# A two-layer graph attention and mixture-of-experts kernel: layer 1's sum over two experts issued in two halves, the planning and padding of the last slots issued in four pieces, and layer 1's two-expert slots moved forward among the last

## The chip, the cores and the metric

The kernel runs on one core of a Trainium2 chip. The metric is the time of one execution on the device in microseconds (us), and the time before is the median of three runs. A profile, taken by the hardware profiler in one further execution, gives the start and length of each instruction, what ended each wait, and the clock that TensorE was granted. The engines are PE (TensorE, matrix products), DVE (VectorE), ACT (ScalarE), POOL (GpSimd) and SP (SyncE, which here does nothing but start transfers).

## The reference, cut to what matters

The input is x, 128 graphs of 64 nodes with 256 features (8192 tokens), and an adjacency matrix of 64 x 64 for each graph. Two layers follow each other, and each has two halves:

```
x = x + elu(attention(layernorm(x), adj))    # inside each graph of 64 nodes
t = layernorm(x)
p = top-2 of the router's 8 scores of t, weights normalised over the two
x = x + (t, in layer 0 alone) + sum over the two experts e of p[e] * ffn_e(t)
```

The experts' hidden width is 256 with gelu in layer 0 and 512 with relu in layer 1. All is float32. Each token goes through only two of eight experts, and which two is known only when the router has run. So the kernel sorts tokens into one list per expert in DRAM as it goes.

## The kernel before

**Blocks.** Tokens are handled in blocks of 512, 16 in a layer, 32 in all. A block runs through `attend` (attention) and then `route` (router and scatter of its rows into the experts' lists). Both are Python generators: every `yield` marks a point at which the program's main loop may turn to something else. `a(i, n)` takes n steps of block i's `attend`, `r(i, n)` n steps of its `route`.

**Slots.** The experts' work goes in slots of 256 rows of one list. A slot has three steps: `x()` turns its rows round on PE (px, L764) and copies them (xT, DVE L768); `h()` is the first layer (ph, PE L846, then ACT L855); `y()` the second (py, PE L877, then DVE L884 adds the bias into ys). py has a single buffer, so the next `y()` on PE waits for DVE's L884 of the slot before. In layer 0 POOL then scatters ys to DRAM (L893). In layer 1 `weighted()` lets ACT scale it (L919) and POOL adds it onto the output rows in DRAM (L922); two adds that could meet on one row must not overlap, so each slot's adds wait until those of the slot before have landed.

**Plans.** After a block's rows are in the lists, `plan` works out on DVE which experts have 256 rows waiting and hands out four slots. At three points, block 8 and block 15 of layer 0 and block 15 of layer 1, the lists end: `fill_up` appends 256 rows of padding to each of the eight lists (eight SP transfers, L526), and `rests` (L604 to L669, some 35 small DVE instructions) plans the remainder as twelve slots: eight of one expert, and seven lists' ends of 128 rows, taken in twos: three slots of two experts (called pair slots here) and a last one of a single half. A pair slot needs two sets of weights and its two halves are added one after the other. The twelve are taken in the order whole, whole, pair, whole, whole, pair, whole, whole, pair, whole, whole, single.

**Buffers and queues.** Weights of experts (wc) have four buffers, and SP loads them ahead (`ahead`, `weights`). Fetches of a slot's rows (`fetch`) go on SP too. Every engine runs its own instructions in the order in which the program issued them; for SP, PE, DVE and ACT that order is exactly the order of these lines (`manual_schedule`), so the main loop (from L1037 on) decides it. One pass of the loop carries block n = t+1 through attention, block t through routing, block t+2 through the start of attention, and four slots through h, y and x.

**Where the first parts stand.** In layer 1 the first step of `attend` adds the two experts' results of layer 0 to xs, with eight scalar_tensor_tensor instructions (L267, 128 x 256 each). In the loop this step of block t+2 comes as `a(t + 2)` just before a `y()`, and behind that stands `a(n)`, block n's normalisation of the softmax (erc and ee, L334 and L335), whose result PE turns round as pp (L339). From pp come pT_bd (DVE L341, ACT L342) and po (PE L348). In the last step of `route` stand `plan`, `fill_up` and `rests` together.

Of the kernel before, what the change touches and what calls it, by code (L numbers as in the profile page):

```python
# [9 lines left out]
I32 = mybir.dt.int32  # L10
# [6 lines left out]
P = 128  # L17
# [3 lines left out]
E = 8  # L21
TT = 4
# [5 lines left out]
ST = SL // P  # L28
# [7 lines left out]
def adj_ffn_kernel(  # L36
# [34 lines left out]
    nc = tc.nc  # L71
    N = x.shape[0]
    NT = N // P
    NB = N // TB
# [6 lines left out]
    SF = SR + E - 1  # L81
# [44 lines left out]
    for g in range(2):  # L126
        r = slice(g * NG, (g + 1) * NG)
# [132 lines left out]
    def attend(l, b, blk):  # L260

        name = f"g{l}_{b}"
        xs, yb, ai = blk["in"]
        if l > 0:
            for t in range(TT):
                for k in range(2):
                    nc.vector.scalar_tensor_tensor(  # L267
                        xs[:, t, :],
                        yb[:, t, k * D : (k + 1) * D],
                        cs[:, b * TT + t, k : k + 1],  # L270
                        xs[:, t, :],
                        ALU.mult,
                        ALU.add,
                    )
        yield
        stats = ln_stats(xs, name)

        m = work.tile([P, TT, NG], F32, tag="cap", name=f"cap_{name}")
# [123 lines left out]
    def route(l, b, blk):  # L402
# [106 lines left out]
        if b - (CUT if b >= CUT and l == 0 else 0) >= LAG:  # L509
            slots.take(l, b, SB, plan(l, f"p{l}_{b}", SB))  # L510
        if b == NB - 1 or (l == 0 and b == CUT - 1):
            fill_up(l, b)
            slots.take(l, b, SF, rests(l, f"p{l}_{b}r"), True)


    def fill_up(l, b):

        bi = small.tile([P, E], I32, tag="bi", name=f"bi{l}_{b}")
        nc.vector.tensor_copy(bi, base[l])
        wr = []  # L520
        for e in range(E):
            r = nc.values_load(
                bi[0:1, e : e + 1], engines=[SP], min_val=0, max_val=E * CAP - SL,
                skip_runtime_bounds_check_because="a list ends within its room",
            )
            ins = nc.sync.dma_start(  # L526
                out=lists[l][bass.ds(r, SL), :].rearrange("(t p) d -> p t d", p=P),
                in_=pad[:, :, 0 : ROW[l]],
            )
            unordered(f"lists{l}", ins)  # L530
            wr.append(ins)
        written[l].append(wr)
        filled[l].extend(wr)
# [71 lines left out]
    def rests(l, name):  # L605

        lf = small.tile([P, E], F32, tag="lf", name=f"lf_{name}")  # L610
        nc.vector.scalar_tensor_tensor(lf, done[l][:, 0:E], -float(SL), base[l], ALU.mult, ALU.add)
        ns = waiting(lf, name)
        nc.vector.tensor_scalar(lf, lf, float(P), None, ALU.subtract)
        pairs = waiting(lf, f"{name}p")
        cc = small.tile([P, 2 * E], F32, tag="cc", name=f"cc_{name}", bufs=1)
        nc.vector.tensor_scalar(cc[:, 0:E], pairs, 2.0, None, ALU.mult)
        nc.vector.tensor_tensor(cc[:, E : 2 * E], ns, pairs, ALU.subtract)
        cum = small.tile([P, 2 * E], F32, tag="cum2", name=f"cum_{name}", bufs=1)
        summed_up(cum[:, 0:E], cc[:, 0:E], f"{name}p")
        summed_up(cum[:, E : 2 * E], cc[:, E : 2 * E], name)  # L620
        nc.vector.tensor_scalar(
            cum[:, E : 2 * E], cum[:, E : 2 * E], cum[:, E - 1 : E], None, ALU.add
        )
        np_ = small.tile([P, 1], F32, tag="np", name=f"np_{name}", bufs=1)
        nc.vector.tensor_scalar(np_, cum[:, E - 1 : E], 0.5, None, ALU.mult)

        at = small.tile([P, SF], F32, tag="hat", name=f"hat_{name}", bufs=1)
        nc.vector.scalar_tensor_tensor(at, sful, np_, snum, ALU.min, ALU.add)
        ge = work.tile([P, SF, 2 * E + 1], F32, tag="ee", name=f"ge_{name}")
        nc.vector.tensor_tensor(  # L630
            ge[:, :, 0 : 2 * E],
            cum.unsqueeze(1).to_broadcast([P, SF, 2 * E]),
            at.unsqueeze(2).to_broadcast([P, SF, 2 * E]),
            ALU.is_le,
        )
        vs = small.tile([P, SF], F32, tag="vs", name=f"vs_{name}", bufs=1)
        nc.vector.tensor_reduce(vs, ge[:, :, 0 : 2 * E], AX.X, ALU.add)

        w = small.tile([P, 2 * E + 1], F32, tag="w2", name=f"w_{name}", bufs=1)
        nc.vector.tensor_tensor(w[:, 0 : 2 * E], cc, cum, ALU.subtract)  # L640
        for i in range(2):
            wi = w[:, i * E : (i + 1) * E]
            nc.vector.scalar_tensor_tensor(wi, done[l][:, 0:E], 2.0, wi, ALU.mult, ALU.add)
        nc.vector.tensor_tensor(w[:, E : 2 * E], w[:, E : 2 * E], cc[:, 0:E], ALU.add)
        nc.vector.tensor_scalar(
            w[:, 2 * E : 2 * E + 1], done[l][:, E : E + 1], 2.0, -2.0 * SR, ALU.mult, ALU.add
        )
        nc.vector.tensor_tensor(
            ge,
            eidx.unsqueeze(1).to_broadcast([P, SF, 2 * E + 1]),  # L650
            vs.unsqueeze(2).to_broadcast([P, SF, 2 * E + 1]),
            ALU.is_equal,
        )
        nc.vector.tensor_tensor(
            ge, ge, w.unsqueeze(1).to_broadcast([P, SF, 2 * E + 1]), ALU.mult
        )
        us = small.tile([P, SF], F32, tag="us", name=f"us_{name}")
        nc.vector.tensor_reduce(us, ge, AX.X, ALU.add)
        tab = small.tile([P, 2, SF], I32, tag="tab", name=f"tab_{name}", bufs=5)
        nc.vector.tensor_tensor(tab[:, 0, :], us, at, ALU.add)  # L660
        es = small.tile([P, SF], F32, tag="es", name=f"es_{name}", bufs=5)
        nc.vector.tensor_scalar(es, vs, float(E), -float(E), ALU.is_ge, ALU.mult)
        nc.vector.tensor_tensor(es, es, vs, ALU.add)
        nc.vector.tensor_scalar(tab[:, 1, :], es, float(E - 1), None, ALU.min)
        took(l, ns, name)
        bu = small.tile([P, E], F32, tag="bu", name=f"bu_{name}")
        nc.vector.tensor_scalar(bu, done[l][:, 0:E], float(SL), None, ALU.mult)
        base[l] = bu
        return es, tab, sum(written[l], [])  # L669

    def fetch(sl, name):

# [16 lines left out]
    class Slots:  # L689
# [10 lines left out]
        def take(self, l, b, n, plan, rest=False):  # L700
            es, tab, ins = plan

            slots = [[(s, slice(0, ST))] for s in range(SR if rest else n)]
            if rest:
                for i, s in enumerate(range(SR, n, ST)):
                    of = [(s + t, slice(t, t + 1)) for t in range(min(ST, n - s))]
                    slots.insert((ST + 1) * i + ST, of)
            for of in slots:
                self.all.append(
                    {"l": l, "of": of, "es": es, "tab": tab, "filled": ins, "wc": [],  # L710
                     "part": part(b), "sums": list(summed), "rest": rest,
                     "st": of[-1][1].stop}
                )
                self.need.extend((len(self.all) - 1, s) for s, _ in of)
# [260 lines left out]
    def a(i, n=1):  # L975
        if there(i):
            for _ in range(n):
                next(blks[i]["a"], None)

    def r(i, n=1):  # L980
# [12 lines left out]
    load(2)  # L993
    load_router()
    load(FIRST)
    a(0, 2)
    make_gw(0)
    a(0)
    a(1, 2)
    token2 = counted("token2", [P, NT], [[2 * P, NT]], 0, 2)  # L1000
    token = counted("token", [P, NT], [[P, NT]], 0, 1)
    place = counted("place", [P, ST], [[P, ST]], 0, 1)
    att = lambda b: [(a, b)] * 9 + [(a, b, 2), (a, b)]
    chains = [
        (0, att(0)[3:] + [(r, 0)] * 10),
        (1, att(1)[2:] + [(r, 1)] * 10),
        (2, att(2) + [(r, 2)] * 9),
        (8, att(3) + [(r, 3)] * 2),
        (12, [(a, 4)] * 3),
    ]  # L1010
    turn = 0
    while any(c for _, c in chains):
# [20 lines left out]
            for l in range(2):  # L1033
                rest_of_lists(l)
        turn += 1
    r(2)
    slots.fetch()  # L1037
    slots.ahead()
    for t in range(FIRST, len(blks)):
        n = t + 1  # L1040
        more = slots.nf - slots.ny > SB or len(slots.all) - slots.ny > SB
        if t + 3 != NB:
            load(t + 3)
        a(n)
        h()
        x()
        a(n)
        r(t - 1)
        a(n)
        h()  # L1050
        r(t)
        slots.fetch()
        if more:
            x()
        a(n)
        r(t)
        if t + 2 != NB:
            a(t + 2)
        y()
        a(n)  # L1060
        (h if more else x)()
        r(t)
        a(n)
        y()
        a(t + 2, 1 + (t + 2 == NB))
        if more:
            x()
        a(n)
        r(t)
        x()  # L1070
        h()
        a(n)
        if more:
            y()
        x()
        a(n)
        h()
        r(n)
        y()
        a(t + 2)  # L1080
        r(t)
        r(t)
        y()
        slots.fetch()
        x()
        r(n)
        r(t)
        if t + 3 == NB:
            load(t + 3)
# [4 lines left out]
    while slots.ny < len(slots.all):  # L1094
        h()
        x()
        y()
        slots.fetch()
    slots.weighted()

# [46 lines left out]
```

## Time and profile before

| what | value |
|---|---|
| median of 3 runs | 1414.73 us (1414.56 to 1415.14) |
| profiled execution | 1416.24 us |
| its span, first to last instruction | 1414.4 us |
| mean granted clock of PE | 0.941 |
| PE, DVE, ACT, POOL busy | 1215.8, 872.8, 646.5, 742.8 us |
| PE's wait for ee (L335) in front of pp | 38.0 us, 19 times |
| PE's wait for sm (L301) in front of pe | 15.6 us, 4 times |
| PE's longest wait in front of ph (L846) | 7.4 us |
| weights of an expert, 512 KB, issue to landing | 4.9 us |
| DMA traffic | 311.69 MB, 220 GB/s |

A row of the timeline reads: start, length, engine, line, operation, result<-operands, partitions x elements, how many instructions are drawn together, and in brackets how long the engine stood idle before and what ended it. A list of waits has: who waited, for whom, us in all, times, the longest. The row PEclk gives the granted clock in tenths for 40 equal slices of the span.

### The profile page before, as it was taken

How to read it: one execution, taken by the hardware profiler on the slowest of the kernel's cores; microseconds unless marked ns; L12 is line 12 of the kernel's file. 1: busy time of each engine (PE TensorE's matmuls, PEld its weight loads, DVE VectorE, ACT ScalarE, POOL GpSimd, SP SyncE). 2: the span in 40 equal slices, each digit the busy share in tenths (PEclk: the TensorE clock that was granted, in tenths of full speed). 3: DMA queues.
4: the chain of work that ended last, by engine and by line, in shares of the span. 5: the costliest groups of instructions: out<-in, count | busy, mean ns of one | idle time of the engine just before them, and what ended most of it. 6: DMA issues, size and time to landing. Idle time of an engine off the chain costs nothing. (4 is left out here: it accounts for less than half of the span.)

```text
span 1414.4 us, 22289 instructions
## 1 busy us (share of the span) xinstructions
PE 1215.8 (86%) x6240; PEld 1046.3 (74%) x6240; DVE 872.8 (62%) x3390; ACT 646.5 (46%) x1550; POOL 742.8 (53%) x729
## 2 busy tenths in 40 slices
PE   6756799879899887888899999999999999799992
PEld 4645677768787776776788787887878887688882
DVE  3565677877667777767766656766567654523330
ACT  5534556546556544544544454344544444233330
POOL 3153576646666654566545664556645556533323
PEclk9767899989999998999999999999999999999997
DMA  6626567797777978778789887798877777888883
GB/s 198 184 86 191 184 206 235 222 264 235 229 236 222 305 253 249 235 220 273 253 246 265 228 244 202 207 264 228 249 189 216 216 193 205 246 226 227 223 225 34
DMA packets 262829, 311.69 MB, mean 220 GB/s; under 512 B 40615, under 2 KB 219950, under 8 KB 262704
## 3 DMA queue, kind: packets, MB, share of 16 engines
q1 hardware_dynamic: 219552, 225.02, 52.7%
q0 software_dynamic: 43152, 85.24, 22.5%
q8 instruction: 50, 0.82, 0.3%
q14 instruction: 75, 0.61, 0.1%
HBM read 212.25 MB, written 99.75 MB: 221 GB/s over the span
## 5 line engine op out<-in xcount | busy, mean ns | idle before, releaser
L877 PE MATMUL py_s<-wc_s,hT_s 128*128 128x256 f32 x1648 | 402.3, 394 | 31.6 <-issue 22.1
L846 PE MATMUL ph_s<-xT_s,wc_s 128*128 128x256 f32 (+1 forms) x1760 | 384.8, 371 | 19.2 <-DVE xT_s L768 9.1
L877 PEld LDWEIGHTS py_s<-wc_s,hT_s 128*128 128x128 f32 x1648 | 314.4, 197 | 81.6 <-issue 24.8
L922 POOL DMA_INDIRECT out_dram<-ys_s,to_s x135 | 213.2, 1579 | 289.5 <-ACT ys_s L919 150.6
L846 PEld LDWEIGHTS ph_s<-xT_s,wc_s 128*128 128x128 f32 x1760 | 317.6, 192 | 64.1 <-DVE xT_s L768 15.4
L499 POOL DMA_INDIRECT lists<-tn_r,ix_r x256 | 248.8, 972 | 97.0 <-issue 65.8
L855 ACT ACTIVATE hT_s<-ph_s,wc_s 128x256 f32<-128x256 f32 (+1 forms) x440 | 174.5, 456 | 143.5 <-PE ph_s L846 90.6
L884 DVE TENSOR_TENSOR ys_s<-py_s,wc_s 128x512 f32<-128x512 f32 (+1 forms) x149 | 97.3, 653 | 171.2 <-PE py_s L877 170.3
L893 POOL DMA_INDIRECT res<-ys_s,to_s x142 | 144.4, 1017 | 106.7 <-DVE erc_g L334 36.5
L768 DVE COPY xT_s<-px_s 128x512 f32<-128x512 f32 (+1 forms) x140 | 95.3, 681 | 93.4 <-PE px_s L764 93.2
L290 PE MATMUL pw_g<-gw,xt_g 128*128 128x258 f32 x512 | 126.2, 397 | 20.0 <-DVE xt_g L255 13.1
L290 PEld LDWEIGHTS pw_g<-gw,xt_g 128*128 128x128 f32 x512 | 96.6, 197 | 41.3 <-issue 13.0
L919 ACT ACTIVATE ys_s<-ys_s,cf_s 128x256 f32<-128x256 f32 x135 | 61.3, 499 | 104.1 <-DVE ys_s L884 103.9
L240 ACT ACTIVATE tn_r<-xb_g,nb_r,rs_r 128x256 f32<-128x256 f32 x128 | 66.4, 589 | 87.3 <-DVE nb_r L238 87.3
L240 ACT ACTIVATE xn_g<-xs,nb_g,rs_g 128x256 f32<-128x256 f32 x128 | 66.4, 589 | 75.4 <-DVE nb_g L238 75.3
L764 PE MATMUL px_s<-ident,xg_s 128*128 128x128 f32 x554 | 86.9, 281 | 6.4 <-DMA xg_s<-lists 3.7
L764 PEld LDWEIGHTS px_s<-ident,xg_s 128*128 128x128 f32 x554 | 71.3, 147 | 20.2 <-DMA xg_s<-lists 3.8
L279 POOL TENSOR_SCALAR cap_g<-adj 128x256 f32<-128x256 int32 x32 | 35.7, 1116 | 85.8 <-DMA adj<-in_adj_dram 51.7
L348 PE MATMUL po_g<-wh_g,pT_bd 128*128 128x256 f32 x256 | 69.4, 418 | 8.3 <-ACT pT_bd L342 6.8
L297 ACT COPY wh_g<-pw_g 128x258 f32<-128x258 f32 x128 | 47.7, 374 | 58.6 <-PE pw_g L290 57.9
L419 PEld LDWEIGHTS pl_r<-rw,xt_r 128*128 128x128 f32 x512 | 68.8, 209 | 5.3 <-ACT xt_r L257 2.9
L342 ACT COPY pT_bd<-pp_g 64x256 f32<-64x256 f32 x32 | 11.6, 363 | 131.1 <-DVE pT_bd L341 131.0
(503 smaller groups left out, 1612.6 us busy)
## 6 DMA issues: line engine op xcount, KB each, us to landing
wc_s<-in_w_dram SPq DMA_DIRECT2D x142, 512.0 KB, 4.9
wc_s<-in_w_dram SPq DMA_DIRECT2D x156, 256.0 KB, 4.2
xg_s<-lists SPq DMA_DIRECT2D x64, 260.0 KB, 3.2
xg_s<-lists SPq DMA_DIRECT2D x64, 258.0 KB, 4.4
yb<-res SPq DMA_DIRECT2D x16, 1024.0 KB, 12.3
wc_s<-bcat SPq DMA_DIRECT2D x78, 129.0 KB, 4.0
wc_s<-bcat SPq DMA_DIRECT2D x71, 130.0 KB, 5.7
xs<-in_x_dram SPq DMA_DIRECT2D x16, 512.0 KB, 6.2
```

The costliest lines, as they stand in the source:

```text
L240: nc.scalar.activation(outs(t), xb[:, t, :], AF.Identity, bias=nb[:, t : t + 1], scale=rs[:, t : t + 1])
L290: nc.tensor.matmul(pw, lhsT=xt[:, k, t * P : (t + 1) * P], rhs=gw[l][:, k, :], start=(k == 0), stop=(k == KD - 1),)
L348: nc.tensor.matmul(po[h][:, j, :], lhsT=pT[:, 2 * h + j, :], rhs=wh[:, 2 * h + j, 0:D], start=True, stop=True,)
L499: ins = nc.gpsimd.indirect_dma_start(out=lists[l], out_offset=bass.IndirectOffsetOnAxis(ap=ix[:, k, t : t + 1], axis=0), in_=tn[:, t, 0 : ...
L764: nc.tensor.transpose(px[:, c, t * P : (t + 1) * P], xg[:, t, c * P : (c + 1) * P], ident)
L768: nc.vector.tensor_copy(xT[:, :, 0 : st * P], px[:, :, 0 : st * P])
L846: nc.tensor.matmul(ph[:, j, r], lhsT=w[:, o : o + P], rhs=xT[:, c, r], start=(c == 0), stop=(c == KD - 1),)
L855: nc.scalar.activation(hT[:, f + j, r], ph[:, j, r], AF.Gelu if l == 0 else AF.Relu, bias=w[:, OB1[l] + f + j : OB1[l] + f + j + 1],)
L877: nc.tensor.matmul(py[:, t, :], lhsT=hT[:, f, t * P : (t + 1) * P], rhs=w[:, O2[l] + f * D : O2[l] + (f + 1) * D], start=(f == 0), stop=(f ...
L884: nc.vector.tensor_tensor(ys[:, r, :], py[:, r, :], w[:, OB2[l] : OB1[l]].unsqueeze(1).to_broadcast([P, r.stop - r.start, D]), ALU.add,)
L893: ins = nc.gpsimd.indirect_dma_start(out=res[sl["part"]], out_offset=self.row(sl, t), in_=ys[:, t, :], in_offset=None, bounds_check=2 * N - 1,
L922: ins = nc.gpsimd.indirect_dma_start(out=out, out_offset=self.row(sl, t), in_=ys[:, t, :], in_offset=None, compute_op=ALU.add,)
```

## The change

The first step of `attend` is split: the sum's eight instructions come in two groups of four with a `yield` between. Where the next block is one of layer 1, the loop issues block n's erc and ee between the groups, ahead of the `y()` that followed the sum; the second group follows that `y()`.

`fill_up` now takes two experts at a time, and `rests` yields four times, so that planning and padding come in four pieces, each a DVE piece and two fills on SP. The loop takes these pieces with `r(t - 1)` at five more places, spread over the pass that follows the block's routing; the slots are handed out after the fourth. After the last block a `r(len(blks) - 1)` stands behind each `y()`.

In layer 1 the twelve slots are now taken in the order whole, pair, whole, pair, whole, pair, whole, whole, whole, whole, whole, single. In layer 0 their order is as before.

```diff
@@ attend
-        if l > 0:
-            for t in range(TT):
+        for i in range(2):
+            for t in range(TT * l * i // 2, TT * l * (i + 1) // 2):
                 for k in range(2):
                     nc.vector.scalar_tensor_tensor(
...
-        yield
+            yield
         stats = ln_stats(xs, name)
@@ route, last step
-            fill_up(l, b)
-            slots.take(l, b, SF, rests(l, f"p{l}_{b}r"), True)
+            bi = small.tile([P, E], I32, tag="bi", name=f"bi{l}_{b}")
+            nc.vector.tensor_copy(bi, base[l])
+            yield
+            for e, at in zip(range(0, E, 2), rests(l, f"p{l}_{b}r")):
+                fill_up(l, bi, range(e, e + 2))
+                yield
+            slots.take(l, b, SF, (*at, sum(written[l], [])), True)
@@ rests
         nc.vector.tensor_tensor(cc[:, E : 2 * E], ns, pairs, ALU.subtract)
+        yield
         cum = small.tile([P, 2 * E], F32, tag="cum2", name=f"cum_{name}", bufs=1)
...
         nc.vector.scalar_tensor_tensor(at, sful, np_, snum, ALU.min, ALU.add)
+        yield
         ge = work.tile([P, SF, 2 * E + 1], F32, tag="ee", name=f"ge_{name}")
...
         nc.vector.tensor_reduce(vs, ge[:, :, 0 : 2 * E], AX.X, ALU.add)
+        yield
...
-        return es, tab, sum(written[l], [])
+        yield es, tab
@@ Slots.take
-                    slots.insert((ST + 1) * i + ST, of)
+                    k = (ST + 1) * i + ST if l == 0 else 2 * i + 1 if len(of) > 1 else len(slots)
+                    slots.insert(k, of)
@@ main loop
         a(n)
         r(t)
+        early = n < len(blks) and blks[n]["l"] == 1
         if t + 2 != NB:
             a(t + 2)
+        if early:
+            a(n)
         y()
-        a(n)
+        r(t - 1)
+        if t + 2 != NB:
+            a(t + 2)
+        if not early:
+            a(n)
         (h if more else x)()
         r(t)
         a(n)
         y()
-        a(t + 2, 1 + (t + 2 == NB))
+        r(t - 1)
+        a(t + 2, 1 + 2 * (t + 2 == NB))
...
         h()
+        r(t - 1)
         a(n)
         if more:
             y()
         x()
+        r(t - 1)
         a(n)
         h()
         r(n)
         y()
         a(t + 2)
+        r(t - 1)
         r(t)
...
@@ after the loop
         x()
         y()
+        r(len(blks) - 1)
         slots.fetch()
```

The lines left out of the diff only let the start-up before the loop take one more step of `attend` at a time, as it now has one `yield` more.

More of the change, by code (lines that the diff above doesn't have):

```diff
@@ L511, in route, with fill_up @@
         if b == NB - 1 or (l == 0 and b == CUT - 1):
-            fill_up(l, b)
-            slots.take(l, b, SF, rests(l, f"p{l}_{b}r"), True)
-    def fill_up(l, b):
-        bi = small.tile([P, E], I32, tag="bi", name=f"bi{l}_{b}")
-        nc.vector.tensor_copy(bi, base[l])
+            bi = small.tile([P, E], I32, tag="bi", name=f"bi{l}_{b}")
[5 more added lines that the diff above has]
+            slots.take(l, b, SF, (*at, sum(written[l], [])), True)
+    def fill_up(l, bi, es):
         wr = []
-        for e in range(E):
+        for e in es:
             r = nc.values_load(
@@ L995, in adj_ffn_kernel @@
     load(FIRST)
-    a(0, 2)
+    a(0, 3)
     make_gw(0)
     a(0)
-    a(1, 2)
+    a(1, 3)
     token2 = counted("token2", [P, NT], [[2 * P, NT]], 0, 2)
@@ L1002, in adj_ffn_kernel @@
     place = counted("place", [P, ST], [[P, ST]], 0, 1)
-    att = lambda b: [(a, b)] * 9 + [(a, b, 2), (a, b)]
+    att = lambda b: [(a, b, 2)] + [(a, b)] * 8 + [(a, b, 2), (a, b)]
     chains = [
@@ L1008, in adj_ffn_kernel @@
         (8, att(3) + [(r, 3)] * 2),
-        (12, [(a, 4)] * 3),
+        (12, [(a, 4, 2), (a, 4), (a, 4)]),
     ]
@@ L1035, in adj_ffn_kernel @@
         turn += 1
-    r(2)
+    r(2, 2)
     slots.fetch()
```

## The prediction

> **What bounds the kernel now.** I read the page's rows 1, 2 and 4 first, then PE's waits, PE's timeline at its longest gaps, the windows of layer 1's regular blocks with DVE and PE side by side in one, and last the chain that ended last, with POOL's tail.
>
> ```profile
> PE 1215.8 (86%) x6240; PEld 1046.3 (74%) x6240; DVE 872.8 (62%) x3390; ACT 646.5 (46%) x1550; POOL 742.8 (53%) x729
> PEclk9767899989999998999999999999999999999997
> ...
> PE pp_g L339 <- DVE ee_g L335: 38.0, 19, 4.2
> PE pe_g L309 <- DVE sm_g L301: 15.6, 4, 5.6
> PE pp_g L339 <- DVE l_r L445: 12.3, 5, 3.1
> PE ph_s L846 <- issue: 7.4, 1, 7.4
> ...
> 307.88 1.22 PE L309 MATMUL pe_g<-sm_g,same 128*128 128x256 f32 x2 [5.59 <-DVE sm_g L301]
> 309.75 3.42 PE L419 MATMUL pl_r<-rw,xt_r 128*128 128x8 f32 x16
> 554.70 1.22 PE L309 MATMUL pe_g<-sm_g,same 128*128 128x256 f32 x2 [5.50 <-DVE sm_g L301]
> 1237.28 5.17 PE L846 MATMUL ph_s<-xT_s,wc_s 128*128 128x256 f32 x16 [7.44 <-issue]
> ```
>
> PE does the work and idles for 14% of the span. Two DVE stretches cause most of what this change can reach. One is the lump of `rests` (L611 to L667, 7.1 us: 300.32 to 307.41), in front of which PE waits 5.59, 5.50 and 7.44 us. The other is the sum over two experts at L267, ahead of erc and ee (L334, L335), for which pp waits:
>
> ```profile
> 943.72 1.03 PE L339 MATMUL pp_g<-ident,ee_g 128*64 128x128 f32 x4 [2.58 <-DVE ee_g L335]
> 944.55 4.71 PE L877 MATMUL py_s<-wc_s,hT_s 128*128 128x256 f32 x16
> ...
> 988.90 0.60 PE L339 MATMUL pp_g<-ident,ee_g 128*64 128x128 f32 x4 [2.70 <-DVE ee_g L335]
> 989.33 3.62 PE L877 MATMUL py_s<-wc_s,hT_s 128*128 128x256 f32 x16
> ...
> 983.86 3.75 DVE L267 SCALAR_TENSOR_TENSOR xs<-yb,cs,xs 128x256 f32<-128x256 f32 x8
> 987.52 0.68 DVE L884 TENSOR_TENSOR ys_s<-py_s,wc_s 128x512 f32<-128x512 f32 x1
> 988.33 0.43 DVE L335 TENSOR_TENSOR ee_g<-ee_g,erc_g 128x256 f32<-128x256 f32 x1
> 991.18 0.41 DVE L341 COPY pT_bd<-pp_g 64x256 f32<-64x256 f32 x1
> ```
>
> The last line carries my main sum: DVE runs without a pause from 980.96 to 991.6, so pT_bd comes at 991.18 whatever stands first among these instructions. Last, the end:
>
> ```profile
> 1361.31 3.47 PE py_s L877 x16
> 1366.05 5.79 DMA out_dram<-ys_s,to_s
> 1386.74 3.85 DMA out_dram<-ys_s,to_s
> 1404.26 3.71 DMA out_dram<-ys_s,to_s
> ```
>
> Up to 1365 the chain runs through PE, then through POOL's scatter-adds (L922), each of which waits until the DMA before it has landed. PE ends at 1390.4, the span at 1414.4.
>
> **The change part by part.** No instruction is added or removed except waits; the work is reordered on DVE, SP and POOL, and on PE only in layer 1's last twelve slots.
>
> *The sum in two halves, nine regular blocks.* After, erc and ee stand behind four of the eight L267s: 983.86 + 4 x 0.47 = 985.74, and 0.6 more make ee ready at 986.3 instead of 988.76. px ends at 986.2, so pp waits some 0.35 us instead of 2.7, and py (3.46) ends at about 990.25 instead of 992.79. But po needs pT_bd, which DVE reaches at 991.18 as before and ACT finishes at 991.99. So po starts at about 992.05: 0.7 us are gained of 2.7, and 1.8 turn into a new wait at po. ys (L884) comes 1.1 us earlier; the second half ends before xT (L768), and the statistics that need it (L227) stand behind the next ys, at 993.60. Now the clock: 943.72 shows 1.03 and 4.71 where 988.90 shows 0.60 and 3.62, thus 1.5 us lost after the same gap. Block windows (pp to pp) show it too: 43.6 to 43.85 us at clock 0.99 to 1.00, 44.9 to 45.2 at 0.97. Three of the seven windows from 767.49 to 1077.68 are slow, 0.64 us per block; gaps of 1.8 and less were mostly without harm (that of 2.06 at 566 was not), so I take back 0.45 of it. 9 x (0.7 + 0.45) = 10.3 us. From below: 0, if another instruction on DVE slides; from above 9 x 3.1 = 28, if pT_bd came early too.
>
> [...]
>
> *The remaining blocks of layer 1.* pp at 601, 641, 681 and 720 waits 3.12, 2.97, 2.92 and 1.84 us (DVE l_r L445), that at 523 4.18. Done by hand with the new order I get 1 us at 523, 2.3 at 601 (1.6 of it the clock), 1.5 for 641 to 720 together and 0.5 at the last: 5.3.
>
> *The lump at block 8 of layer 0 (300 us).* It is cut in pieces of 1.70, 1.45, 0.82 and 3.15 us; 1.70 lies behind a ys, the others in places up to 30 us later. pe loses its 5.59 wait and pT comes at 311.9 instead of 320.22. But the last three pieces (5.4 us) lie on DVE's unbroken run to a later ys, for which PE's next py (L877, 330.09) waits: that py now starts at 327.15, so 2.9 us remain, with a gap of some 5.6 in front of it. That gap turns the clock cold as the old one did. The nearest row for its price is 1237.28: 5.17 instead of 3.62, 1.55 us. 2.9 - 1.5 = 1.4. From above 10 (the whole gap and the 4 us of slow pl and py behind it), from below -1.
>
> *The lump at block 15 of layer 0 (547 us).* In the same way: po 6.2 earlier, but the py behind it 577.7 instead of 579.18; 1.5 less a cold 1.5 = 0 (from -3 to +7).
>
> *SP.* Eight pad fills (260 KB each, 6.3 us to landing at the tail) were issued in one burst behind the plan; now four fetches and a weight load come ahead, and fills go in pairs between weight loads. In layer 0 later weights are needed more than 10 us after they land; I cost it at nothing; without that cover one 512 KB load (4.9 us) would stand on PE's path once. In the tail seven fetches wait for the last fills to land, and the first rest slot's weights are queued behind them; by my schedule they land some 2 us before they are needed. POOL: the layer norm's L232 moves ahead of an L922 pair, and L499 and L893 change places in two blocks; POOL is 53% busy, and its 25 us of 44 per block leave room: nothing.
>
> *The tail.* PE's gap of 7.44 falls to some 0.9, and ph takes 3.6, not 5.17: PE gains 8.1. The end is the scatter-adds' chain, however. Its next add goes out at 1247.89, behind the lists' L499s and two adds at 1235 and 1237; at best it goes at 1243. Against that 4.9, the eight fills now lie beside these adds rather than in PE's idle time (a step takes 6.4 us in quiet, 7.0 to 9.5 with transfers), for which I charge 1.2. Gain 3.7 (0 to 8).
>
> *Pair slots earlier (W W P W W P... becomes W P W P W P W W W W W S).* Twelve slots and fifteen steps as before: W1 at 1308.59 to S at 1408.75, 100.2 us. A pair costs 16.0 and 14.2 us in traffic, the last one 9.2 in quiet; that one moves into traffic (+5), a whole slot out of it (9.5 to 6.4, -3). With four weight buffers, two pairs' second weights come only after the pair before is half done, some 2.8 us of PE each, and the chain stands 14 to 17 us behind PE, so that hides. I charge 0.9 net; if the lag did not cover it, 5.6 more.
>
> Sum: 10.3 + 5.3 + 1.4 + 0 + 3.7 - 0.9 = 19.8. The profiled execution took 1416.24 (span 1414.4 and 1.8 around it); 1396.4. The median of the runs lies 1.5 under it: 1394.9.
>
> **The rivals.**
> A, above: 1395; 0.50.
> B, the gaps really vanish: pT_bd early, pieces hidden, the chain follows PE. 10 + 7 + 28 + 5.3, and 8 at the tail: 58; a part of it, 45, is what I give it: 1370. Against it stands DVE's unbroken run. 0.10.
> C, the wait only changes its name: pp's becomes po's to the full 2.7, lumps come out at 0, the chain sets the end. Clock relief 4, early blocks 3, tail 2: 9 us, 1406. For it: pT_bd's fixed place. 0.20.
> D, slower: the tail's weights. Pairs ahead ask for seven sets of weights in four slots rather than five, behind seven fetches that wait for the last fills. If that crowding brings all six steps of the pairs to 9.7 us (the longest in the trace, 1323.93 to 1333.61), the pairs cost 58.2 instead of 39.4, +18.8; with the two weight stalls no longer hidden, +5.6: 24.4 lost against the 20.7 gained elsewhere, 1418.4. It decides once the tail loses over 20.7 us. For it: DMA stands at 0.74 to 0.86 there. Against: the adds' DMA takes 3.8 to 7 us. 0.13.
> E, nothing: new orders on DVE cost elsewhere what they give. 1414; 0.07.
>
> **How the numbers follow.** About 0.2% (2.8 us) is what a measurement of this kernel can tell from no change. Likeliest A, 1394.9. From 1378 (A with its upper bounds at block 8 and in the tail) to 1415 (C, and half of E) it leaves out D and half of B: 2 in 10. Faster 0.79 (A, B, C less a little), same 0.08, slower 0.13.
>
> **What would show it.** Right: PE's waits for ee_g fall from 38 to under 15, and po's for pT_bd (6.8 us now) rise to about 20; regular windows near 42.9 at clock 0.99; no gap at pe, one of 4 to 6 us at a py some 25 us later; the gap of 7.44 gone, and 105 to 108 us from the first rest slot's first add to the span's end (105.8 now). Wrong: regular windows still 43.7 (C), or over 125 us from that add to the end (D), or po without a wait (B).

## The result, and the profile after

The changed kernel takes 1394.64 us (median of four runs, 1391.12 to 1397.4); the kernel before, run with it, 1414.93. The ratio is 0.9856, with a 95% interval of [0.9832, 0.9881]: 20 us less, where 19.8 had been forecast. The sum came out to within a microsecond, but two of its terms had the wrong sign, as the experiments show, and a third was too low: that they cancelled is luck.

The profiled execution took 1397.4 us with a span of 1395.6; it is the slowest of the four, so a sum over its stretches comes to 18.8 us, not 20. Two of the page's rows, and chosen rows of PE's list of waits, after the change:

```profile
PE 1208.4 (87%) x6240; PEld 1035.8 (74%) x6240; DVE 872.5 (63%) x3390; ACT 647.2 (46%) x1550; POOL 742.3 (53%) x729
PEclk9767899999999999998999999999999999999996
...
PE py_s L884 <- issue: 28.6, 29, 5.2
PE po_g L348 <- ACT pT_bd L342: 28.3, 23, 3.0
PE pp_g L339 <- DVE ee_g L335: 16.1, 19, 2.6
PE ph_s L853 <- DMA wc_s<-in_w_dram: 7.6, 4, 3.4
PE pe_g L309 <- DVE sm_g L301: 4.6, 2, 4.1
PE pp_g L339 <- DVE l_r L445: 1.4, 1, 1.4
```

The row for po before:

```profile
PE po_g L348 <- ACT pT_bd L342: 6.8, 10, 1.8
```

pp's two waits fell from 50.3 us to 17.5, and po's wait for pT_bd rose from 6.8 to 28.3: the wait moved one step on, as expected, and lost a part of itself on the way. (Behind the sum the lines have moved by seven: L877, L884 and L922 of before are L884, L891 and L929 here.) One regular block of layer 1, chosen rows of PE and then of DVE, in the timeline:

```profile
973.21 0.60 PE L339 MATMUL pp_g<-ident,ee_g 128*64 128x128 f32 x4 [0.28 <-DVE ee_g L335]
973.72 3.72 PE L884 MATMUL py_s<-wc_s,hT_s 128*128 128x256 f32 x16
978.79 1.56 PE L348 MATMUL po_g<-wh_g,pT_bd 128*128 128x256 f32 x6 [1.35 <-ACT pT_bd L342]
...
970.61 1.91 DVE L267 SCALAR_TENSOR_TENSOR xs<-yb,cs,xs 128x256 f32<-128x256 f32 x4
972.64 0.43 DVE L335 TENSOR_TENSOR ee_g<-ee_g,erc_g 128x256 f32<-128x256 f32 x1
973.58 1.91 DVE L267 SCALAR_TENSOR_TENSOR xs<-yb,cs,xs 128x256 f32<-128x256 f32 x4
976.41 0.18 DVE L445 SCALAR_TENSOR_TENSOR l_r<-oh_r_10a,lg_r 128x32 f32<-128x32 f32 x1
977.93 0.41 DVE L341 COPY pT_bd<-pp_g 64x256 f32<-64x256 f32 x1
```

pp waits 0.28 us where it waited 2.70, and po 1.35 where it did not wait (992.79). From the sum's first instruction to pT_bd it is 7.32 us (970.61 to 977.93), and it was 7.32 before (983.86 to 991.18): DVE has the same list to go through. A window from pp to pp says what a block gained (columns: window, length, busy time of PE, PEld, which is PE loading weights, DVE, ACT and POOL, PE's clock, the busy share of the DMA engines, GB/s). After, and two blocks of before:

```profile
930.14:973.21 43.07, 40.91 (x212) 35.50 (x213) 28.73 (x112) 19.84 (x51) 24.70 (x20) 1.00 0.84 229
```
```profile
811.22:854.92 43.70, 40.58 (x212) 35.53 (x213) 28.89 (x112) 19.82 (x51) 24.95 (x20) 1.00 0.83 232
943.72:988.90 45.18, 41.94 (x213) 36.65 (x214) 28.83 (x112) 19.82 (x51) 24.68 (x20) 0.97 0.84 226
```

Against the undisturbed block (43.70) 0.63 us are gained, against the one with a slow clock (45.18) 2.11. None of the eight regular blocks after the change has a slow pp (0.60 us in each, the clock 1.00).

At layer 0's plan the gap moved from pe to a later py, where the prediction had placed it (327.15 for block 8, first row, and 577.7 for block 15, second row):

```profile
327.08 3.75 PE L884 MATMUL py_s<-wc_s,hT_s 128*128 128x256 f32 x8 [5.19 <-issue]
574.32 3.20 PE L884 MATMUL py_s<-wc_s,hT_s 128*128 128x256 f32 x8 [3.85 <-issue]
```

The span divides into three at pp of two blocks, and behind the last pp (in the first column, the time of the pp before / after):

| stretch | before | after | gain |
|---|---|---|---|
| up to pp at 767.49 / 758.05 (layer 0, early blocks of layer 1) | 767.49 | 758.05 | 9.4 |
| eight regular blocks, to pp at 1121.33 / 1102.24 | 353.84 | 344.19 | 9.65 |
| one more, to the last pp at 1164.73 / 1144.87 | 43.40 | 42.63 | 0.8 |
| behind the last pp (the tail) | 249.67 | 250.73 | -1.1 |

So the loop gave 19.9, and the tail, from which 2.8 had been expected, took 1.1 more. These are one execution each, and the four executions of the changed kernel lie 6 us apart, so the ratios further down weigh more than this row. PE and POOL in the tail show why it is no better (of POOL, the first of a slot's two adds, rows chosen; before below after):

```profile
1264.32 5.38 PE L853 MATMUL ph_s<-xT_s,wc_s 128*128 128x256 f32 x16 [3.37 <-DMA wc_s<-in_w_dram]
...
1227.35 1.56 POOL L929 DMA_INDIRECT out_dram<-ys_s,to_s  x1 [4.75 <-ACT hT_s L862]
1237.89 1.55 POOL L929 DMA_INDIRECT out_dram<-ys_s,to_s  x1 [7.11 <-DMA out_dram<-ys_s,to_s]
1248.53 1.55 POOL L929 DMA_INDIRECT out_dram<-ys_s,to_s  x1 [7.23 <-ACT ys_s L926]
1302.48 1.55 POOL L929 DMA_INDIRECT out_dram<-ys_s,to_s  x1 [7.39 <-ACT ys_s L926]
1389.96 1.55 POOL L929 DMA_INDIRECT out_dram<-ys_s,to_s  x1 [3.08 <-DMA out_dram<-ys_s,to_s]
```
```profile
1247.89 1.56 POOL L922 DMA_INDIRECT out_dram<-ys_s,to_s  x1 [9.18 <-ACT ys_s L919]
1256.06 1.55 POOL L922 DMA_INDIRECT out_dram<-ys_s,to_s  x1 [4.75 <-ACT ys_s L919]
1263.35 1.55 POOL L922 DMA_INDIRECT out_dram<-ys_s,to_s  x1 [3.88 <-ACT ys_s L919]
```

The gap of 7.44 is gone from PE, but the adds now go 10.5 us apart (1227.35, 1237.89, 1248.53) where the steps of before there were 8.2 and 7.3 (1247.89, 1256.06, 1263.35). The first rest slot's add goes out at 1302.48, 157.6 us behind the last pp, before 143.9 (1308.59). From there to the last add it is 87.5 us instead of 100.2.

### The profile page after: what moved, and what is told of

Its sections match the earlier page's. It is cut to its first block, busy times and chain, and to the rows that moved or that the text cites. A ratio compares the mean times of both kernels' runs of the same rounds, so it can differ in the third digit from the quotient of the medians.

```text
span 1395.6 us, 22284 instructions
## 1 busy us (share of the span) xinstructions
PE 1208.4 (87%) x6240; PEld 1035.8 (74%) x6240; DVE 872.5 (63%) x3390; ACT 647.2 (46%) x1550; POOL 742.3 (53%) x729
## 5 line engine op out<-in xcount | busy, mean ns | idle before, releaser
L884 PE MATMUL py_s<-wc_s,hT_s 128*128 128x256 f32 x1648 | 393.7, 388 | 39.9 <-issue 28.6
L884 PEld LDWEIGHTS py_s<-wc_s,hT_s 128*128 128x128 f32 x1648 | 306.5, 192 | 88.9 <-issue 31.3
L929 POOL DMA_INDIRECT out_dram<-ys_s,to_s x135 | 213.0, 1578 | 266.3 <-DMA out_dram<-ys_s,to_s 87.6
L891 DVE TENSOR_TENSOR ys_s<-py_s,wc_s 128x512 f32<-128x512 f32 (+1 forms) x149 | 97.1, 651 | 150.9 <-PE py_s L884 145.3
L348 PE MATMUL po_g<-wh_g,pT_bd 128*128 128x256 f32 x256 | 74.2, 440 | 29.8 <-ACT pT_bd L342 28.3
L348 PEld LDWEIGHTS po_g<-wh_g,pT_bd 128*128 128x128 f32 x256 | 53.0, 217 | 47.1 <-ACT pT_bd L342 36.6
```

The lines of the kernel that those rows point to most:

```text
L348: nc.tensor.matmul(po[h][:, j, :], lhsT=pT[:, 2 * h + j, :], rhs=wh[:, 2 * h + j, 0:D], start=True, stop=True,)
L884: nc.tensor.matmul(py[:, t, :], lhsT=hT[:, f, t * P : (t + 1) * P], rhs=w[:, O2[l] + f * D : O2[l] + (f + 1) * D], start=(f == 0), stop=(f ...
L891: nc.vector.tensor_tensor(ys[:, r, :], py[:, r, :], w[:, OB2[l] : OB1[l]].unsqueeze(1).to_broadcast([P, r.stop - r.start, D]), ALU.add,)
L929: ins = nc.gpsimd.indirect_dma_start(out=out, out_offset=self.row(sl, t), in_=ys[:, t, :], in_offset=None, compute_op=ALU.add,)
```

## The experiments

Each was compared with the kernel before on its own chip. Medians of before differ there (1416.28 to 1418.37 us), so ratios are compared; their intervals reach 0.0015 to 0.0036 to either side. Where a run is said to lie some us under or above the changed kernel's ratio, that is the difference of the two ratios times 1416. Of the diffs the lines that matter are shown.

### The three parts one by one

Only the sum in two halves, with erc and ee between (the loop's `early` lines and the split of `attend`):

> The kernel before with the sum over two experts in two halves alone (erc and ee between them); rests in one lump and the slots' order as before. Theory of the prediction: layer 1's blocks gain 0.7 us each through pp, 0.45 through the clock, the early ones some 5 in all: 15 to 17 us less, about 1399, with po's wait for pT_bd some 20 us longer. Rival (the wait only changes its name): 3 to 7 us less, about 1410. Rival (the whole wait goes): over 25 us less.

Measured: 0.9866 [0.9841, 0.9891], 1398.97 us against 1418.37.

```diff
-        if l > 0:
-            for t in range(TT):
+        for i in range(2):
+            for t in range(TT * l * i // 2, TT * l * (i + 1) // 2):
...
+        early = n < len(blks) and blks[n]["l"] == 1
         if t + 2 != NB:
             a(t + 2)
+        if early:
+            a(n)
         y()
-        a(n)
+        if t + 2 != NB:
+            a(t + 2)
+        if not early:
+            a(n)
```

```profile
PE po_g L348 <- ACT pT_bd L342: 28.3, 23, 2.8
...
PE pe_g L309 <- DVE sm_g L301: 15.8, 4, 5.6
PE pp_g L339 <- DVE ee_g L335: 12.5, 19, 1.8
```

This is nearly the whole effect: 19 us of 20 by the ratios, somewhat more than the 15 to 17 expected, and 16.2 at the last pp by its profile (1148.58 against 1164.73). po's 28.3 is that of the changed kernel; pe's 15.8 us stay, as the lump does.

Only `rests` and `fill_up` in pieces:

> The kernel before with rests and fill_up in four pieces alone. Theory: 1.4 us at block 8, 0 to 4 at block 15, and in the tail between +1 and -4, since the chain of scatter-adds sets the end and the fills now lie beside it: 1409 to 1414. Rival (the three gaps of 5.6, 5.5 and 7.4 really vanish): 1393 to 1398. Rival (the fills slow the adds more than PE gains): 1417 or more.

```diff
-            fill_up(l, b)
-            slots.take(l, b, SF, rests(l, f"p{l}_{b}r"), True)
+            for e, at in zip(range(0, E, 2), rests(l, f"p{l}_{b}r")):
+                fill_up(l, bi, range(e, e + 2))
+                yield
```

Measured: 1.0004 [0.9987, 1.0021]. The tail of its profile took 251.6 us behind the last pp, two more than before. By the ratio it is 0.6 us more, from 1.8 less to 3.0 more, where about 1 to 6 less was expected: a miss, at the edge of the interval. The rival in which the gaps vanish is out; the one in which the fills cost more than PE gains (2 us or more above before) lies partly inside the interval.

Only the new order of the pair slots:

> The kernel before with the pair slots of layer 1 moved forward alone. Theory of the prediction: fifteen steps as before, so 0 to +1 us, 1414 to 1416. Rival, read from the changed kernel's trace (from the first rest slot's add to the last 87.5 us instead of 100.2): pairs' second adds lie under PE's work instead of behind it, 8 to 12 us less, about 1404. Rival (weights late with four buffers): 3 to 6 us more.

```diff
-                    slots.insert((ST + 1) * i + ST, of)
+                    k = (ST + 1) * i + ST if l == 0 else 2 * i + 1 if len(of) > 1 else len(slots)
+                    slots.insert(k, of)
```

Measured: 0.9982 [0.9967, 0.9998]: 2.6 us less, from 0.3 to 4.7, where the prediction had a loss of 0.9. Its profiled execution (1409.53) was the fastest of its twelve and so shows more than that: the tail is 243.5 us, and the first rest slot's add to the last takes 93.6 instead of 100.2. Near the end its adds wait for their data (ys_s) rather than for each other, but for the last two (first add of a slot each; the last one, at 1402.02, not shown):

```profile
1372.99 1.56 POOL L923 DMA_INDIRECT out_dram<-ys_s,to_s  x1 [3.47 <-ACT ys_s L920]
1381.18 1.55 POOL L923 DMA_INDIRECT out_dram<-ys_s,to_s  x1 [4.77 <-ACT ys_s L920]
1389.15 1.55 POOL L923 DMA_INDIRECT out_dram<-ys_s,to_s  x1 [4.57 <-ACT ys_s L920]
1395.58 1.55 POOL L923 DMA_INDIRECT out_dram<-ys_s,to_s  x1 [3.02 <-DMA out_dram<-ys_s,to_s]
```

The pairs' double steps came early, the chain caught up with PE (8.2 us a slot) during whole slots, and only the last two steps stand behind it. That is the part of my count that was wrong: I counted steps, not how many of them stand behind PE's last work. Behind the start of PE's last py there are four steps before (1391.35 to 1408.75), and two here (1395.58 and 1402.02).

The changed kernel without that order:

> The changed kernel without the new order of the pair slots. Theory of the prediction: as the changed kernel or 1 us less, 1393 to 1395. Rival (the order is what saves the tail): 5 to 12 us more than the changed kernel, 1399 to 1406.

```diff
-                    k = (ST + 1) * i + ST if l == 0 else 2 * i + 1 if len(of) > 1 else len(slots)
-                    slots.insert(k, of)
+                    slots.insert((ST + 1) * i + ST, of)
```

Measured: 0.9869 [0.9844, 0.9894], that is 18.6 us less than before. Against the changed kernel's 0.9856 that is 1.8 us more, less than the intervals tell apart. In the changed kernel the adds lag, and four steps stand behind PE's last py again (1367.40; adds at 1370.64 to 1389.96).

### Where the tail's gain went

Layer 1's plan and fills at once again:

> The changed kernel, but after the last block rests and all eight fills are issued at once as before; layer 0's pieces, the sum and the slots' order stay as changed. Theory (in the tail the pieces lay the fills beside the adds and delay the first rest slot's weights, which costs what the new order gives): the loop as in the changed kernel, the tail as in the run with the order alone (243.5 us behind the last pp instead of 250.7): 5 to 7 us less than the changed kernel, about 0.981 of before. Rival (the prediction's: pieces gain in the tail): 3 to 8 us more than the changed kernel.

```diff
-    r(len(blks) - 1)
+    r(len(blks) - 1, 7)
     slots.fetch()
     h()
```

Measured: 0.9806 [0.9778, 0.9833], 7.1 us under the changed kernel's ratio (the intervals touch only at their ends). Its profiled execution, the slowest of its six, has a tail of 247.5 us. PE gets its gap of 7.4 back, and it is faster none the less (first add of a slot each):

```profile
1216.51 1.59 POOL L929 DMA_INDIRECT out_dram<-ys_s,to_s  x1 [0.30 <-issue]
1230.61 1.56 POOL L929 DMA_INDIRECT out_dram<-ys_s,to_s  x1 [10.62 <-ACT ys_s L926]
1238.19 1.55 POOL L929 DMA_INDIRECT out_dram<-ys_s,to_s  x1 [4.15 <-ACT ys_s L926]
1245.66 1.55 POOL L929 DMA_INDIRECT out_dram<-ys_s,to_s  x1 [4.05 <-ACT ys_s L926]
```

After one step of 14.1 us they are 7.5 apart. Where the fills stand shows in SP's timeline, first of this run, then of the changed kernel:

```profile
1211.60 8.66 SPq L529 DMA_DIRECT2D lists<-pad  x8
1221.96 3.06 SPq L688 DMA_DIRECT2D xg_s<-lists  x4
```
```profile
1220.54 3.03 SPq L688 DMA_DIRECT2D xg_s<-lists  x4
1226.16 1.28 SPq L529 DMA_DIRECT2D lists<-pad  x2
1241.95 1.29 SPq L529 DMA_DIRECT2D lists<-pad  x2
1251.01 5.78 SPq L688 DMA_DIRECT2D xg_s<-lists  x7
```

With the lump the fills go out while PE has nothing to do and POOL issues its last scatters into the lists and one pair of adds (1216.51); the next add comes at 1230.61. In pieces the plan's four fetches stand in front of them and wait for the last rows of the lists (7.5 us on SP's queue), and from 1211 to 1220 the DMA is busy for 0.30 only; with the lump it is busy for 0.9 or more there, in slices of 2.75 us. The fills follow from 1226 on, the burst of seven fetches behind them, all beside the adds. From 1219.1 to 1265.1 the changed kernel's DMA is busy for 0.97, and a weight load's median to landing between 1190 and 1300 is 7.6 us; with the lump (1216.5 to 1261.5) 0.83, and 4.7.

All profiles agree on this. The eight steps from the second add behind the lists' last scatter to the first rest slot's add (1227.35 to 1302.48 in the changed kernel) take 59 to 61 us in the six kernels with the lump in the tail, and 72 to 75 in the four with the pieces as changed.

To separate the transfers from the DVE pieces, all fills with the first piece:

> The changed kernel, but in the tail all eight fills go out with the first piece; the DVE pieces stay spread over four slots. Theory (it is the fills' transfers beside the adds that slow the tail's first adds to 8 to 10 us): the steps behind the first go back to 7 to 8 us and the tail falls from 250.7 to about 244 to 246, 5 to 7 us less than the changed kernel, 0.981 of before. Rival (DVE's pieces or the late fetches and weights do it): within 2 us of the changed kernel.

```diff
-                fill_up(l, bi, range(e, e + 2))
+                if l == 0 or e == 0:
+                    fill_up(l, bi, range(e, e + 2 if l == 0 else E))
```

Measured: 0.9838 [0.9802, 0.9873]. Its tail is 245.4 us, as expected, but steps of 9.4, 10.0 and 9.1 us remain, and the ratio's interval holds the theory (0.981) and all of the rival's range (0.984 to 0.987). Inconclusive: the fills still stood behind the four fetches here (1232.68), so this run moved them less than meant.

The first rest slot's weights ahead of the seven fetches:

> The changed kernel, but in the tail the first rest slot's weights are requested ahead of the burst of seven fetches. Theory (these weights are late because they stand behind fetches that wait for the last fills): PE's wait of 3.4 us for wc at the first rest slot and its cold 5.4 go; but the adds' chain sets the end, so 0 to 3 us less than the changed kernel. Rival (they are late since DMA is full, wherever they stand): the wait stays over 2 us.

```diff
         r(len(blks) - 1)
+        slots.ahead()
         slots.fetch()
```

Measured: 0.9859 [0.9825, 0.9894], the same as the changed kernel. PE's waits for wc in the tail fall from 6.4 us to 3.2, and at the first rest slot (ph at 1260.22) there is none, so the order of the queue made the weights late. The time doesn't answer, within 5 us, as it is the adds that set the end. The eight steps named above take 64 us with the fills first and 65 with the weights first: each brings back a good part, neither all of it (one execution each, that of weights_first its fastest).

### What held the rest of the wait

> The changed kernel with one DVE step moved in layer 1: the eight small instructions L445 to L450 (1.5 us) behind pT_bd (L341). Theory (pT_bd's fixed place on DVE is what keeps the gain of a block at 0.7 of 2.7 us): po's wait falls from some 28 us to under 12, a regular block from 43.05 to about 41.6, 9 x 1.45 + some 5 in the early ones: 13 to 18 us less than the changed kernel, about 0.975 of before. Rival (another engine sets the block's length by then, POOL or ACT): under 4 us.

```diff
         (h if more else x)()
-        r(t)
+        if not early:
+            r(t)
         a(n)
+        if early:
+            r(t)
         y()
```

Measured: 0.9769 [0.9738, 0.9799], 12.3 us under the changed kernel's ratio, a little less than the 13 to 18 expected. In a regular block po no longer waits, and the block is at PE's own time (40.74 of 41.39 us busy; rows chosen, columns as above):

```profile
963.36 0.60 PE L339 MATMUL pp_g<-ident,ee_g 128*64 128x128 f32 x4
963.86 3.72 PE L884 MATMUL py_s<-wc_s,hT_s 128*128 128x256 f32 x16
967.42 1.99 PE L348 MATMUL po_g<-wh_g,pT_bd 128*128 128x256 f32 x8
...
963.36:1004.75 41.39, 40.74 (x212) 35.51 (x213) 28.68 (x112) 19.84 (x51) 25.03 (x21) 1.00 0.85 246
```

This settles the prediction's main step: it was pT_bd's place in DVE's list that let a block keep only 0.7 of 2.7 us. Moving eight small instructions (1.5 us) past it brings 1.6 a block (331.57 us for the eight regular blocks instead of 344.19).

Layer 0's last three DVE pieces moved further back:

> The changed kernel with the last three DVE pieces of rests in layer 0 issued together at the end of the pass, behind the next block's router step instead of ahead of L362 and L365; the fills and the first piece stay where they are. In the tail they come together at the fifth step. Theory (in the pass the pieces lie on DVE's unbroken run to ys, and past it DVE has pauses): py's gap of 5.2 us at 327 and of 3.9 at 574 goes, 5 to 8 us less than the changed kernel. Rival (the pieces cost the same wherever they stand): within 1 us of it.

```diff
@@ rests: the next block's base is set with the first piece, the rest follows in one
+        was = done[l]
+        took(l, ns, name)
+        bu = small.tile([P, E], F32, tag="bu", name=f"bu_{name}")
+        nc.vector.tensor_scalar(bu, done[l][:, 0:E], float(SL), None, ALU.mult)
+        base[l] = bu
+        for _ in range(3):
+            yield
         yield
...
@@ main loop: the fifth step of r(t - 1) at the end of the pass
-        r(t - 1)
         r(t)
         r(t)
...
         r(n)
         r(t)
+        r(t - 1)
         if t + 3 == NB:
```

Measured: 0.9889 [0.9861, 0.9917], 4.7 us above the changed kernel's ratio, where 5 to 8 less were expected; the intervals overlap, so no loss is shown, but the gain is absent. The gap at py goes, and another opens at the next layer norm's product:

```profile
330.44 5.41 PE L290 MATMUL pw_g<-gw,xt_g 128*128 128x258 f32 x16 [3.34 <-DVE xt_g L255]
```

From the pp ahead of block 8's plan to the second behind it the changed kernel takes 69.19 us (278.49 to 347.68) and this run 67.81: 1.4 are gained, not 5. The four blocks behind take 141.05 us instead of 136.08. The rest slots are handed out later here, which changes the order of the work on PE in these blocks; that this is the cause is argued, as no run separates it. In the tail, too, this run takes the pieces together, one slot later: behind the last pp it takes 246.5 us instead of 250.7. A third place for the same 5 us, and the third with a gap.

The three together:

> The three together: layer 1's rests at once, L445 to L450 behind pT_bd, layer 0's last pieces at the end of the pass. Theory: the gains add, 23 to 32 us less than the changed kernel, 0.963 to 0.969 of before. Rival (one hides another): under 15 us less than the changed kernel.

Measured: 0.9788 [0.9755, 0.982], so the gains do not add: with the third part it is no faster than pt_first alone (0.9769). Without it:

> The changed kernel with layer 1's rests and fills at once (as in lump_tail) and L445 to L450 behind pT_bd (as in pt_first). Theory: the two gains add, 12 + 7 us less than the changed kernel, 0.972 of before, about 1376. Rival (a shorter loop only brings forward the adds' chain that then sets the end): 0.976 to 0.978.

Measured: 0.9701 [0.9671, 0.9732], 1373.7 us (1370.24 to 1374.77) against 1416.28: 42 us under the kernel before, and 1.6% under the changed kernel's ratio. The edits are the diffs of lump_tail and pt_first, no more; the two gains (7.1 and 12.3) add, and the third part costs 12 us in the run above. It is the lowest of all versions.

With the fills first and the weights first in place of the lump:

> fills_first, weights_first and pt_first together. Theory: 12 + 6 + 1 us less than the changed kernel, 0.972 of before, like best2 but without PE's gap of 7.4 us in the tail, so up to 3 us less than best2. Rival (the adds' chain sets the end of both): the same as best2.

Measured: 0.9708 [0.9676, 0.974], the same as best2. PE has no gap of 7.4 us there, but one of 3.5, and the time is no shorter: again the adds set the end (PE's last py starts at 1356.38, the last add at 1373.50).

## Why the prediction was right or wrong, point by point

**The sum in two halves: right, mechanism and size.** 1.15 us a block had been said; eight blocks gave 9.65, 1.21 each. The wait at pp is 0.28 (0.35 said), that at po 1.35 (1.8 said). The run with this part alone, and pt_first for the reason, show it. The clock's term was 0.45 a block. Three of these eight blocks were slow by 1.5 us before (pp 1.03 us and py 4.57 to 4.73 where the others have 0.60 and 3.62), none after: 0.56. In the two other kernels with the sum in one piece (pieces_only, order_only; mean clock of the profiled execution 0.944 and 0.943) four and three of them are slow, in the runs with the sum in halves none (pp 0.60 us; mean clock 0.950 in sum_only). The gap's length alone does not decide it: the slow blocks had gaps of 2.58 to 2.76 us in front of pp, the others of 2.59 to 2.72.

**The early blocks: right in the sum.** In the run with the sum alone, pp of the first regular block comes 5.85 us earlier (761.64, not 767.49); 6.0 had been forecast (4.8, and 1.15 for one block more). Singly they are off both ways: up to pp at 521.57 2.3 us are gained (1 said), from there to 598.86 0.8 (2.3 said).

**Layer 0's lumps: right at block 8, too low at block 15.** The places of the new gaps were right (327.08 for 327.15, 574.32 for 577.7). From the pp ahead of block 8's plan to the second behind it, the run with the sum alone takes 70.91 us and the changed kernel 69.19: 1.7, where 1.4 was said. From 486.26 to 598.86 and from 483.76 to 594.94, over block 15's, 112.60 and 111.18: 1.4, where 0 was said. 0.6 of it lies ahead of the plan and is unexplained. Behind it, py starts 55.89 us behind pp at 518.43, against 57.63 behind pp at 521.57 with the sum alone: 1.7 us earlier, where 1.5 was said. The mis-sized term is the price of the gap in front of py: 1.5 was charged, and 0.8 of the 1.7 are left at pp at 594.94, so it was 1.0, with a gap of 3.85 us. At block 8 (gap 5.19) the price was near: of 3.5 us by which py starts earlier than in the kernel before (48.59 us behind that pp, not 52.08), 1.8 are left at the second pp behind and 1.7 gone (1.55 said). py takes 3.75 instead of 1.97 there, px 1.06 instead of 0.60.

**The tail's pieces: wrong in sign.** Step: "Gain 3.7 (0 to 8)". The reason given, the adds' chain sets the end, is right. The first term was right: the next add was to come 4.9 us sooner, and it does by 4.4 (8.23 us behind the one before it instead of 12.66). The term that failed is the 1.2 us for fills beside the adds: the eight steps that follow took 75.1 us instead of 60.7, 14 more. The last slots win back 9 us of that: from the first rest slot's add to the last it is 87.5 us, against 96.6 in lump_tail with the same order of slots. On balance lump_tail shows 7 us for the pieces' being there, by intervals that just touch. In "SP" I had listed that four fetches go ahead of the fills and priced it at nothing; but those fetches wait for the lists' last rows, and the fills behind them thereby miss the time in which the DMA is mostly idle (busy for 0.30 from 1211 to 1220).

**The weights of the first rest slot: wrong, without consequence.** "They land some 2 us before they are needed" was 3.4 us late (PE's wait at 1264.32). The adds' lag hid it, as far as weights_first can tell.

**The order of pair slots: wrong in sign.** Step: "that one moves into traffic (+5), a whole slot out of it (9.5 to 6.4, -3)". order_only gives 2.6 us less. The steps behind PE's last work count: four before, two with the order alone. In the changed kernel no run tells its effect from nothing (1.8 us).

The errors offset: the loop gave 19.9 where 17.0 was forecast, the tail -1.1 where +2.8 was. Of the signs named beforehand, the waits for ee fell to 16.1 us (under 15 said), po's rose to 28.3 (about 20 said), and from the first rest slot's add to the span's end it is 93.1 us, not 105 to 108: that sign was missed. **Rivals:** E (nothing) is outside the interval. B (gaps vanish) fell by po's 28.3 us; C by the 9.65 us of the regular blocks, of which it had only the clock's part; D's crowding was there, with steps of up to 10.8 us (9.7 had been set), but on the slots ahead of the pairs, and the tail lost 1.1 us where 20.7 were needed.

What stays open: in the tail, how much of the 7 us is the fills' transfers and how much the burst of fetches and the weights behind them. fills_first left the fills behind the four fetches, and its interval, like that of weights_first, is too wide.

## What to carry to other kernels

Moving work out from in front of a waiting engine gained here only up to the next result that the same queue still had to deliver (0.63 of 2.7 us in a block at full clock): look for the last instruction of the unbroken run, not at the wait. Where that result stands behind work nobody waits for, move that work, as pt_first did (1.6 us a block). A transfer that waits in an issue queue can keep later ones out of a stretch in which the DMA has room: four fetches waited up to 7.5 us on SP's queue, and the fills behind them went out from 1226.16 on, past a stretch with the DMA at 0.30. And in this chain of dependent steps those behind the last computation counted, so put the double ones early; here that was worth 2.6 us, and only where the chain did not lag anyway.

## What the runs showed of the hardware that was not expected

Two gaps of nearly the same length had cold stretches of different length. The clock in the windows behind the gap of 5.59 us before the change (pl with 8 columns, then py), and behind the 5.19 after it (py, px, pt, ph):

```profile
311.00:314.00 3.00, 3.00 (x13) 2.84 (x13) 0.69 (x4) 3.00 (x12) 0.00 (x0) 0.50 1.01 185
314.00:317.00 3.00, 3.00 (x9) 2.34 (x8) 0.63 (x4) 0.30 (x1) 0.00 (x0) 0.50 0.93 277
```
```profile
327.00:330.00 3.00, 2.92 (x7) 2.41 (x8) 2.22 (x17) 2.07 (x4) 2.44 (x3) 0.50 0.66 183
330.00:333.00 3.00, 3.00 (x15) 2.71 (x15) 1.96 (x6) 0.34 (x1) 1.89 (x2) 0.58 0.81 266
333.00:336.00 3.00, 3.00 (x18) 2.63 (x17) 1.04 (x3) 2.93 (x7) 2.09 (x4) 1.00 0.96 265
```

In the first case the window before these, from 307.80, also had 0.50: over 9 us at half the clock, against some 5. Both times PE was busy without a pause. At block 15 before (pe at 554.70, gap 5.50) it was the same, 0.50 up to 564. With wide products alone behind the gap the cold stretch varied: some 3 us at 1237.28 before (gap 7.44, ph 5.17 us), some 6 at 1218.50 in lump_tail (gap 7.38, ph 6.68 us), both worked out from ph's 3.62 us at full clock and a clock of 0.50 behind the gap. Both stretches of over 9 us hold pl's narrow products; no run shows whether these set the length. And a scatter-add's step, 6.4 us with DMA at 0.37 (1370.64 to 1377.02), took 10.5 us (1227.35 to 1237.89) in a stretch with DMA at 0.97.
